# A buffer of zeros taken ahead of the first loads, and a copy of the turned sums cut in two

## The chip, the cores and the metric

One of the eight cores of a Trainium2 chip runs the whole kernel. The metric is the device time in microseconds (us), and the time before is the median of three runs. A core has five engines with a queue each: TensorE (PE, with its weight loads shown apart as PEld), VectorE (DVE), ScalarE (ACT), GpSimd (POOL) and SyncE (SP), which here only issues transfers. An engine takes its instructions in the order of its queue; engines wait for each other through semaphores.

## The reference

The kernel computes one layer of a Perceiver in float32: 256 latent tokens of width 512 read a context of 25,088 tokens of the same width, then attend to themselves, and then go through a mixture of 64 experts with a shared one. Cut to what matters here:

```python
qp = layernorm(x) @ Wq.T + bq           # 256 x 128
kp = ctx @ Wk.T + bk                    # 25088 x 128
z  = sigmoid(qp @ kp.T / sqrt(128))     # 256 x 25088
x  = x + z @ (ctx @ Wv.T + bv)
x  = x + attention(layernorm(x))        # 16 heads, causal
x  = x + experts(layernorm(x))          # top 8 of 64, and a shared expert
```

The kernel sums `z @ ctx` first and multiplies by `Wv.T` once at the end, so the sums over the context (called `zc`, 256 x 512) have to be turned (transposed) before that last product.

## The kernel before, in words

**Stages.** The context is read in 66 groups: group 0 has 128 tokens, the others 384 (three blocks of 128). The steady loop over the groups takes the span from about 23 us to 556 us. After it come the turn of the sums and the product with `Wv` (to about 566 us), the self-attention (to about 623 us), and the experts (to the end).

**A group.** For group g, `load_context` (L125) brings the tokens into a `ctx` tile (five buffers in a ring) and `load_quarters` (L115) brings them once more in four transfers, laid out so that one instruction of VectorE, `turn` (L315), makes the transposed `cT`. `keys` (L345) makes `kT` from `cT` on TensorE, `scores` (L365) makes the sigmoid `zT`, and `values` (L558) multiplies `zT` with the context into six PSUM banks `xacc`. That product runs through a scheme with fewer multiplications than the plain one; its sums and differences `S` and `T` are made by VectorE, GpSimd and ScalarE. Groups 0 and 1 are turned by TensorE instead (`turn_by_pe`, L319, tile `ptc`), because there is no time yet for the other layout.

**The start.** SyncE issues, in this order: half of `x`, `ctx` of group 0, `wk_plain`, `ctx` of group 1, four `quarters` of group 2, four parts of `wkT`, `ctx` of group 2, and then the groups that follow. Its later transfers wait for earlier ones to land, and, once the buffers are used up, for a buffer to come free. When `x` is there, VectorE computes mean and variance (`bn_stats`, L256), the reciprocal (L585) and the normalised `xn` in two halves of 128 tokens (L587). TensorE then turns `ctx` of group 0 (L332), turns `xn` (`pt_xn`, L598, eight transposes), makes the keys of group 0 (`pk`, L353) and the queries (`pq`, L611).

**The products of zeros.** `keep_warm(3)` (called at L581) multiplies a buffer of zeros `idle_sb` by itself three times; in float32 each product is two instructions, so six `pi` matmuls of 128 x 512. They stand first in TensorE's queue. The buffer of zeros is one of the five `ctx` buffers, filled by a memset of VectorE (L241).

**Order.** A scheduler may move instructions of an engine's queue unless they are wrapped in `in_turn`, which holds them in the order of the program among each other. The memset of L241 and the products of `keep_warm` are not wrapped. In the program the memset stands behind the loads and the constants and ahead of the statistics of `x`; in the queue of VectorE that the scheduler made it stands behind both halves of `xn`.

**The turn of the sums.** After the last group VectorE combines the banks into `zc` (L684), whose last thirds come one after another. `turn_zc(t, ...)` (L696) turns the half `t` of `zc`: four transposes on TensorE into a PSUM bank `pt_zc` (L700), then one copy of 128 x 512 by ScalarE into `zcT` (L705). `project_values` (L722) multiplies `zcT` with `Wv`, two instructions for each of the four chunks c. The calls stand in this order, which `in_turn` keeps:

```python
turn_zc(0, sum_bank)
project_values(0, range(0, 2))
turn_zc(1, sum_bank)
project_values(0, range(2, ND))
project_values(1, range(ND))
```

Of the kernel before, what the change touches and what calls it, by code (L numbers as in the profile page):

```python
# [9 lines left out]
F32 = mybir.dt.float32  # L10
# [4 lines left out]
P = 128  # L15
# [6 lines left out]
def tile_perceiver_layer(  # L22
# [25 lines left out]
    nc = tc.nc  # L48

    T, D = x.shape  # L50
# [9 lines left out]
    ND = D // P  # L60
    NI = I // P
    J = 3
# [13 lines left out]
    cpool = cross.enter_context(tc.tile_pool(name="cpool", bufs=2))  # L76
# [5 lines left out]
    def keys_bank(name):  # L82
        return psum.tile([P, 512], F32, tag="keys", name=name)
# [3 lines left out]

    def sum_bank(name):
        return pacc.tile([P, 512], F32, tag="acc", name=name)

# [104 lines left out]
        17: [fetch_lnog, fetch_lnob, fetch_gates],  # L197
    }


    ident = const.tile([P, P], F32, tag="ident", name="ident")
    make_identity(nc, ident)
# [33 lines left out]
    eps2_sb = const.tile([P, 1], F32, tag="eps2", name="eps2_sb")  # L236
    nc.vector.memset(eps2_sb, EPS * EPS)


    idle_sb = cpool.tile([P, J, D], F32, tag="ctx", name="idle_sb", bufs=5)[:, 0, :]  # L240
    nc.vector.memset(idle_sb, 0.0)  # L241

    def keep_warm(n):
        pi = keys_bank("pi")
        for _ in range(n):
            nc.tensor.matmul(pi, lhsT=idle_sb[:, 0:P], rhs=idle_sb, start=True, stop=True)

    in_turn = tc.keep_in_program_order  # L250

    def moments(src, nm, twice=False):

# [65 lines left out]
    def turn_by_pe(g):  # L319

        cT = new_turned(g)
        blocks = blocks_of(g)
        n = len(blocks)

        many = 512 // (n * P)
        for lo in range(0, ND, many):
            pt = sum_bank(f"ptc_{g}_{lo}")[:, 0 : many * n * P]
            for c in range(lo, lo + many):
                for i, k in enumerate(blocks):
                    at = ((c - lo) * n + i) * P  # L330
                    in_turn(
                        nc.tensor.transpose(  # L332
                            pt[:, at : at + P],
                            ctx_tiles[g][:, k, c * P : (c + 1) * P],
                            ident,
                        )
                    )
            to = cT[:, lo : lo + many, 0 : n * P // R, :]
            src = pt.rearrange("p (c b r) -> p c b r", c=many, r=R)
            if lo % 2:  # L340
                in_turn(nc.vector.tensor_copy(to, src))
            else:
                in_turn(nc.scalar.copy(to, src))
# [140 lines left out]
    def open_products():  # L484
        for i, names in enumerate(PRODUCTS):
            held = sum_bank(f"xacc_{i}")
            banks_of_products.append(held)
            at = 0
            for text in names:
                nm = text.split()[0]  # L490
                width = (WIDTH if nm in WIDE else WIDTH - 2) + (nm in WITH_ONES)
                product[nm] = (i, slice(at, at + width))
                at += width
            assert at <= 512
# [3 lines left out]
    for i in range(2):  # L498
        t = cpool.tile([P, NT_SUMS, WIDTH + 2], F32, tag=f"T{i}", name=f"T_{i}", bufs=1)
# [58 lines left out]
    def values(named, lo=0, hi=15):  # L558
# [7 lines left out]
        for i, (nm, lhs, rhs), last in made[lo:hi]:  # L566
# [12 lines left out]
            opened.add(i)  # L579

    keep_warm(3)  # L581
    xn = work.tile([P, NT, D], F32, tag="tok", name="xn")
    found = [moments(x_sb[:, t, :], f"x{t}") for t in range(NT)]
# [7 lines left out]
    turn_by_pe(0)  # L591
    xnT = work.tile([P, ND, T], F32, tag="tokT", name="xnT")
    pxs = [sum_bank(f"pt_xn_{c}") for c in range(0, ND, 2)]
    for t in range(NT):
        for c in range(ND):
# [13 lines left out]
    for c in range(ND):  # L609
# [3 lines left out]
                lhsT=wqT_sb[:, c, :],  # L613
                rhs=xnT[:, c, :],
                start=(c == 0),
                stop=(c == ND - 1),
# [45 lines left out]
    for i in range(len(PRODUCTS) - 1):  # L662
        n = max(cols.stop for b, cols in product.values() if b == i)
# [12 lines left out]
    for line in RESULTS.strip().splitlines():  # L676
        to, x_, op, y_ = line.split()
        a_, b_, o_ = result(x_), result(y_), result(to)
        n = widths[to] = min(widths[x_], widths[y_])
        assert to not in ("c01", "c11") or n == WIDTH  # L680
        if to[0] == "c" and to[2] != "1":
            n = WIDTH - 2
# [11 lines left out]
    zcT = work.tile([P, ND, T], F32, tag="tokT", name="zcT")  # L694

    def turn_zc(t, where):  # L696
        pt = where(f"pt_zc_{t}")
        for c in range(ND):
            in_turn(
                nc.tensor.transpose(  # L700
                    pt[:, c * P : (c + 1) * P], zc[:, t, c * P : (c + 1) * P], ident
                )
            )
        in_turn(
            nc.scalar.copy(  # L705
                zcT[:, :, t * P : (t + 1) * P], pt.rearrange("p (c q) -> p c q", c=ND)
            )
        )

    turn_zc(0, sum_bank)  # L710
    x1 = act.tile([P, NT, D], F32, tag="x1", name="x1")
    for t in range(NT):
# [21 lines left out]
# [5 lines that stand above are left out]
# [827 lines left out]
```

## Time and profile before

| What | Value |
|---|---|
| Median of three runs | 792.94 us (791.81 to 792.98) |
| The profiled execution's own time | 792.2 us |
| Its span on the core | 790.3 us |
| TensorE busy | 769.8 us (97% of the span) |
| VectorE, ScalarE, GpSimd busy | 548.3, 202.3, 154.4 us |
| Moved by DMA | 140.86 MB |

The span runs from the first to the last instruction of the profiled execution; 1.9 us of its time lie outside it. Times inside the span, such as 8.28 us, are counted from its start. "Busy" of TensorE includes the products of zeros.

### The profile page before, as it was taken

Reading aid. Unit: us, or ns where it says so; the run is one execution under the profiler, and the core shown is the slowest. Engines: PE = TensorE matmul, PEld = TensorE weight load, DVE = VectorE, ACT = ScalarE, POOL = GpSimd, SP = SyncE. Lnnn points to the kernel's source line nnn. Section 1 sums busy time; section 2 is a strip of 40 time slices with the busy share of each in tenths; the row PEclk is TensorE's granted clock in tenths of the full one; section 3 lists DMA queues with packets and bytes.
Section 4 is the critical chain, followed back from the end, with each engine's and each line's share of the span. In section 5 each row is a group of like instructions: output and inputs, shape, how many; then the busy total and the mean of one; then the engine's idle time right before and its main releaser. Section 6 shows DMA issues by size and latency. Waiting matters only on the chain.

```text
span 790.3 us, 12132 instructions
## 1 busy us (share of the span) xinstructions
PE 769.8 (97%) x4004; PEld 611.3 (77%) x4004; DVE 548.3 (69%) x1596; ACT 202.3 (26%) x483; POOL 154.4 (20%) x304
## 2 busy tenths in 40 slices
PE   5999999999999999999999999999999999999996
PEld 4788888888888888888888888888675586775562
DVE  3888887888878888788887888877656563513222
ACT  3322222222222222222222222222535210110110
POOL 2123232222322223222232222322124000000000
PEclk9999999999999999999999999999999999999999
DMA  9989999999879787786787878840510043399400
GB/s 247 254 213 229 269 230 270 224 230 219 190 181 213 170 210 187 187 209 169 210 186 185 209 171 208 187 121 1 193 47 2 1 133 121 122 353 391 158 1 30
DMA packets 153653, 140.86 MB, mean 178 GB/s; under 512 B 9072, under 2 KB 113008, under 8 KB 153584
## 3 DMA queue, kind: packets, MB, share of 16 engines
q1 hardware_dynamic: 152848, 139.49, 69.6%
q8 instruction: 34, 0.56, 0.3%
q10 hardware_dynamic: 672, 0.52, 0.2%
q14 instruction: 35, 0.29, 0.1%
q0 software_dynamic: 64, 0.00, 0.0%
HBM read 139.47 MB, written 0.52 MB: 177 GB/s over the span
## 4 chain that ended last, share of the span: by engine, by line
PE 95%; DVE 2%; ACT 1%; DMA 0%; POOL 0%; issue 0%; ACTq 0%
PE xacc L570 36%; PE pk L353 21%; PE pz L371 11%; PE ph_e L1124 7%; PE pd_e L1171 4%; PE ph_s L1124 3%; PE pd_s L1171 2%; PE pa L839 2%; PE ph_few L1393 1%; PE pw L903 1%; PE py L725 1%; PE ps L929 1%; PE ptp L980 1%; PE po_few L1424 1%; PE pf L1370 1%; PE pd_few L1438 1%
## 5 line engine op out<-in xcount | busy, mean ns | idle before, releaser
L570 PE MATMUL xacc<-T,S 128*128 128x172 f32 (+2 forms) x912 | 185.5, 308 | 0.0
L353 PE MATMUL pk<-cT,wkT_sb 128*128 128x384 f32 x512 | 175.5, 486 | 0.0
L570 PEld LDWEIGHTS xacc<-T,S 128*128 128x128 f32 x912 | 152.6, 190 | 20.3
L353 PEld LDWEIGHTS pk<-cT,wkT_sb 128*128 128x128 f32 x512 | 97.1, 190 | 54.4
L537 DVE TENSOR_TENSOR T<-ctx 128x172 f32<-128x172 f32 (+1 forms) x262 | 113.5, 434 | 0.0
L317 DVE STREAM_TRANSPOSE cT<-quarters 128x1536 f32<-128x1536 f32 x64 | 113.3, 1770 | 0.0
L537 POOL TENSOR_TENSOR T<-ctx 128x172 f32<-128x172 f32 x65 | 32.0, 493 | 391.3 <-PE xacc L570 373.5
L371 PE MATMUL pz<-qT,kT 128*128 128x256 f32 x392 | 106.0, 379 | 0.7 <-ACT kT L362 0.7
L537 DVE TENSOR_TENSOR S<-zT 128x128 f32<-128x128 f32 x196 | 56.2, 287 | 72.7 <-ACT zT L380 72.7
L380 ACT ACTIVATE zT<-pz 128x256 f32<-128x256 f32 (+1 forms) x131 | 64.2, 490 | 114.0 <-PE pz L371 114.0
L570 PE MATMUL xacc<-T,zT 128*128 128x173 f32 (+1 forms) x396 | 89.9, 308 | 0.0
L570 PE MATMUL xacc<-ctx,S 128*128 128x172 f32 x392 | 78.5, 309 | 0.0
L537 DVE TENSOR_TENSOR S<-zT,S 128x128 f32<-128x128 f32 x325 | 76.3, 284 | 0.0
L362 ACT ACTIVATE kT<-pk,bk 128x384 f32<-128x384 f32 (+1 forms) x66 | 38.2, 578 | 146.9 <-PE pk L353 146.9
L547 ACT COPY T<-ctx 128x170 f32<-128x170 f32 (+1 forms) x130 | 43.2, 334 | 125.4 <-PE xacc L570 125.4
L537 POOL TENSOR_TENSOR T<-ctx,T 128x170 f32<-128x170 f32 (+1 forms) x130 | 72.4, 576 | 2.2 <-PE xacc L570 2.2
L371 PEld LDWEIGHTS pz<-qT,kT 128*128 128x128 f32 x392 | 68.6, 190 | 4.8 <-ACT kT L362 1.3
L537 DVE TENSOR_TENSOR T<-ctx,T 128x172 f32<-128x172 f32 x195 | 65.5, 361 | 8.2 <-PE xacc L570 1.5
L570 PEld LDWEIGHTS xacc<-T,zT 128*128 128x128 f32 x396 | 66.4, 190 | 0.1
L570 PEld LDWEIGHTS xacc<-ctx,S 128*128 128x128 f32 x392 | 62.8, 190 | 0.0
L570 PE MATMUL xacc<-ctx,zT 128*128 128x170 f32 (+1 forms) x264 | 59.5, 307 | 0.0
L1124 PE MATMUL ph_e<-fT,gu 128*128 128x256 f32 x256 | 57.9, 381 | 0.0
(237 smaller groups left out, 713.2 us busy)
## 6 DMA issues: line engine op xcount, KB each, us to landing
ctx<-in_context SPq DMA_DIRECT2D x65, 768.0 KB, 5.3
quarters<-in_context SPq DMA_DIRECT2D x256, 192.0 KB, 6.3
gu<-in_e_gate_up SPq DMA_DIRECT2D x12, 1024.0 KB, 8.9
dn<-in_e_down SPq DMA_DIRECT2D x11, 512.0 KB, 7.0
gu_s<-in_s_gate_up SPq DMA_DIRECT2D x8, 512.0 KB, 6.4
a_wqT<-in_a_wqT SPq DMA_DIRECT2D x1, 2048.0 KB, 12.4
a_wout<-in_a_woutT SPq DMA_DIRECT2D x1, 2048.0 KB, 10.6
dn_s<-in_s_down SPq DMA_DIRECT2D x4, 512.0 KB, 7.8
```

The costliest lines, as they stand in the source:

```text
L317: in_turn(nc.vector.transpose(new_turned(g), q.rearrange("p b (c r) -> p c b r", r=R)))
L353: nc.tensor.matmul(pk, lhsT=w[:, c, :], rhs=cT[:, c, 0 : n // R, :].rearrange("p b r -> p (b r)"), start=(c == 0), stop=(c == ND - 1),)
L362: in_turn(nc.scalar.activation(kT[:, 0:n], pk, AF.Identity, bias=bk_sb))
L371: nc.tensor.matmul(pz[:, i * T : (i + 1) * T], lhsT=kT[:, at : at + P], rhs=qT, start=True, stop=True,)
L380: nc.scalar.activation(zT[:, blocks[0] : blocks[-1] + 1, :].rearrange("p j t -> p (j t)"), pz[:, 0 : len(blocks) * T], AF.Sigmoid, scale=1 ...
L537: in_turn(f(o_, a_, b_))
L547: in_turn(nc.scalar.copy(named[to][:, 0:n], named[x_][:, 0:n]))
L570: nc.tensor.matmul(banks_of_products[i][:, cols], lhsT=named[lhs], rhs=named[rhs][:, 0:n],  start=i not in opened, stop=(g == G - 1 and last),
L725: nc.tensor.matmul(pys[t], lhsT=zcT[:, c, t * P : (t + 1) * P], rhs=wvT_sb[:, c, :], start=(c == 0), stop=(c == ND - 1),)
L839: nc.tensor.matmul(pa[:, 0 : hi - lo], lhsT=a_wqT_sb[:, c, e * P : (e + 1) * P], rhs=anT[:, c, lo:hi], start=(c == 0), stop=(c == ND - 1),)
L1124: nc.tensor.matmul(ph[:, f * T + lo : f * T + hi], lhsT=gu[:, c, col : col + P], rhs=fT[:, c, lo:hi], start=(c == 0), stop=(c == ND - 1),)
L1171: nc.tensor.matmul(pd, lhsT=hT[:, f, t * P : (t + 1) * P], rhs=dn[:, f, :], start=(f == 0), stop=(f == NI - 1),)
```

## The change

Two edits. In the first, the buffer of zeros is taken from the ring of `ctx` buffers, and filled, at the head of the kernel, before any load of context is stated; the memset and the products of `keep_warm` are now held in the order of the program by `in_turn`. In the second, ScalarE's copy of the turned sums is made in two copies of 128 x 256 instead of one of 128 x 512, for each of the two halves t.

```diff
+    in_turn = tc.keep_in_program_order
+    idle_sb = cpool.tile([P, J, D], F32, tag="ctx", name="idle_sb", bufs=5)[:, 0, :]
+    in_turn(nc.vector.memset(idle_sb, 0.0))
...
+    def keep_warm(n):
+        pi = keys_bank("pi")
+        for _ in range(n):
+            in_turn(
+                nc.tensor.matmul(pi, lhsT=idle_sb[:, 0:P], rhs=idle_sb, start=True, stop=True)
+            )
...
-    idle_sb = cpool.tile([P, J, D], F32, tag="ctx", name="idle_sb", bufs=5)[:, 0, :]
-    nc.vector.memset(idle_sb, 0.0)
-
-    def keep_warm(n):
-        pi = keys_bank("pi")
-        for _ in range(n):
-            nc.tensor.matmul(pi, lhsT=idle_sb[:, 0:P], rhs=idle_sb, start=True, stop=True)
-
-    in_turn = tc.keep_in_program_order
...
-        in_turn(
-            nc.scalar.copy(
-                zcT[:, :, t * P : (t + 1) * P], pt.rearrange("p (c q) -> p c q", c=ND)
-            )
-        )
+        pc = pt.rearrange("p (c q) -> p c q", c=ND)
+        for c in range(0, ND, 2):
+            in_turn(
+                nc.scalar.copy(zcT[:, c : c + 2, t * P : (t + 1) * P], pc[:, c : c + 2, :])
+            )
```

In the queues that result, the memset is the first instruction of VectorE, where it was the one behind the second half of `xn`; the order on TensorE, GpSimd and SyncE is the one of before, and ScalarE has four copies of `zcT` where it had two.

## The prediction

> **What bounds the kernel now.** I read the page first. TensorE is busy in nearly every slice of the span, but not in the first.
>
> ```profile
> span 790.3 us, 12132 instructions
> ...
> PE   5999999999999999999999999999999999999996
> ...
> PE 95%; DVE 2%; ACT 1%; DMA 0%; POOL 0%; issue 0%; ACTq 0%
> ```
>
> The second line gives TensorE's busy share in 40 slices of 19.8 us, the third the engines' shares of the chain that ended last. TensorE sets the end nearly everywhere, so time is won where it stands still or does something useless on that chain. The list of TensorE's waits has one that outweighs the rest:
>
> ```profile
> PE pi L246 <- DVE idle_sb L241: 8.3, 1, 8.3
> ```
>
> TensorE waits 8.3 us for the buffer of zeros; the next entry is 0.9 us, and between 25 and 556.5 us the list is empty. So a shift at the start isn't given back to a wait that is in the loop already. The chain of waits of the first 25 us (start us, us, what) shows what stands around it:
>
> ```profile
> 0.76 3.91 DMA x_sb<-in_x
> ...
> 7.14 0.55 DVE xn L587
> 7.68 0.06 issue
> 7.74 0.50 DVE idle_sb L241
> 8.23 0.04 issue
> 8.28 4.72 PE pi L246 x6
> 13.00 0.44 PE ptc L332 x4
> 13.43 0.87 PE pt_xn L598 x8
> 14.31 0.96 PE pk L353 x8
> ```
>
> The real work could start when xn is there, at 7.69. Instead the memset follows xn, the six products of zeros follow the memset, and the first transposes start at about 12.9. The whole 4.72 us of products of zeros lies on the chain. The other edit touches the stretch behind the loop, seen in the timeline (start us, us, engine, line, out<-in):
>
> ```profile
> 557.71 0.70 PE L700 MATMUL pt_zc<-ident,zc 128*128 128x128 f32 x4 [0.70 <-DVE zc L684]
> ...
> 558.45 0.59 ACT L705 COPY zcT<-pt_zc 128x512 f32<-128x512 f32 x1 [1.40 <-PE pt_zc L700]
> ...
> 559.08 1.98 PE L725 MATMUL py<-wvT,zcT 128*128 128x512 f32 x4 [0.68 <-ACT zcT L705]
> ...
> 560.18 0.33 DVE L684 TENSOR_TENSOR zc<-u 128x172 f32<-128x172 f32 x1
> ```
>
> TensorE stands still for 0.68 us while ScalarE copies all four chunks, of which the next four instructions need two.
>
> [...] the first pi products follow each other in 0.85 us, the sixth starts 0.55 us behind the fifth, and the products after it in 0.43 us; if the clock doubled once, it was at 12.1, or 3.83 us after the first. [...] between 556.86 and 559.08 TensorE runs only four transposes, and the products behind them start 0.43 us apart, at full clock.
>
> **Edit 1, the zeros.** Nothing is removed or added but waits; one memset moves from behind xn to the head of VectorE's queue. The queues of SyncE, GpSimd and ScalarE keep their order and waits here, so no transfer is moved past another: ctx of group 4 still is what takes the buffer of zeros over, and it was issued at 19.24, after the buffer had been free for 6 us.
> - Memset: VectorE's first instruction starts at 0.83, so it runs from 0.83 to 1.31 (0.48 us, its row). Behind it stand seven small memsets, done at 1.33 before and then at 1.8; the next work, the statistics of x, waits for x until 4.70. This cover is 2.9 us, so the memset costs nothing.
> - Products of zeros: from 1.37 (the same 0.06 us behind the memset) for 4.72 us, to 6.09, while TensorE would wait anyway.
> - ptc (0.44 us): ctx of group 0 landed at 5.5, so it follows at about 6.0 and ends at 6.5. ScalarE copies it from 6.75 (behind the second square root, which ended at 6.72) to 7.35.
> - pt_xn: the second half of xn is done at 7.69; with 0.14 us from VectorE to a transpose (557.56 to 557.71 in the loop's end) its four transposes start at 7.83, and the last at 8.16. Before, that one started at 14.04. **Shift: 14.04 - 8.16 = 5.88 us.** From there pk, pq and the copies follow in the order and with the gaps of before.
>
> Does the data arrive 5.88 us earlier? The trace's transfers (size, us from issue to landing):
>
> ```profile
> ctx<-in_context SPq DMA_DIRECT2D x1, 768.0 KB, 8.1
> quarters<-in_context SPq DMA_DIRECT2D x1, 192.0 KB, 8.5
> ```
>
> Those are ctx of group 1, issued at 2.15, landing at 10.2, and the last quarter of group 2, issued at 5.21, landing at 13.75. Needed are, in the new times: wk_plain (landed 7.3) at 8.3; ctx of group 1 at 16.83 - 5.88 = 10.95; the quarters of group 2 by the turn at 19.51 - 5.88 = 13.6, which slips by 0.1 us but whose keys are wanted at 18.7, 3 us after it is done; wkT (landed 15.05) at 18.7; ctx of group 2 (17.1) at 18.5; the quarters of group 3 (20.7) at 21.6; those of group 4 (26.3) at 27.9. All are there, by 0.7 us at the closest. None of these issues moves, as they wait for each other; from about 28 us on the issues of before were tied to freed buffers and move along. So all 5.88 us should stay.
>
> **Edit 2, the copies.** One copy of 128x512 (0.59 us) becomes two of 128x256. A row of that shape and engine is there, in the timeline of the experts' part:
>
> ```profile
> 629.74 0.37 ACT L287 COPY fT<-pt_fn 128x256 f32<-128x256 f32 x1 [1.52 <-PE pt_fn L279]
> ```
>
> The first copy still waits for all four transposes (the second has no wait of its own), so the first products start 0.59 - 0.37 = **0.22 us** earlier, at 558.86, and end their issue at 560.68 instead of 560.90. The transposes of the other half need zc, whose last sum ends at 560.51; with 0.14 us, 560.65, so the gain just stays. The second copies end 0.15 us later (2 x 0.37 - 0.59), under 1.7 us of products; for half 1 they end at about 562.1, while its products start at 562.85. Half 0's x1 and all after it follow TensorE. If the last sum comes later, the gain is 0; if TensorE pays for the added waits, up to -0.1 us.
>
> **Sum.** 5.88 + 0.22 = 6.1 us. Against the profiled execution: 792.2 - 6.1 = 786.1. The median of the runs is 0.74 us above that execution. [...] Between 786.1 and 792.94 - 6.1 = 786.8 I take **786.5**.
>
> **The rivals.**
> - *The clock falls back or comes late* (0.13). Between 6.0 and 8.3 TensorE then runs 12 transposes in 2.3 us, where it had dense work before. [...] Against it speaks the stretch at 557 us. The price is 1 us for each us of work at half clock[...]. If it is only late, 0.5 us: 787.0.
> - *The data comes late* (0.03). The closest margin is 0.7 us, while the DMA engines are full until about 31 us. If the loop's start hangs on landings, the whole gain is lost, as if TensorE were at the same place at 25 us: 792.7, no change. Against: the margins above.
> - *The clock stays low: slower* (0.02). Place: pk, pq and the first groups, in the start. To eat 6.1 us and 1.6 us more, 7.7 us of work must run at half clock, i.e. until about 8.3 + 15.4 = 23.7. That is the deciding point; at 30 us it would be 6.1 - 10.9 = -4.8 us, 797.7. Against: the work is dense from 8.3 on, and the clock of before rose after 3.83 us.
> - *The zeros don't come ahead* (0.02): then only 0.22 us remain, 792.7, no change. Against: the memset has no wait and is first in the queue.
>
> **The numbers.** The main case has 0.80, and 785.3 to 787.6. A difference within 0.2% (1.6 us) can hardly be told from no change. Faster: 0.80 + 0.13 + part of the data case, 0.95; same: 0.03; slower: 0.02. The range, 785.2 to 789.3, takes in the main case and most of the clock's.
>
> **What would show it.** Right: pi starts at about 1.4 and pq at 9.2 (15.1 before), the turn of group 3 at 21.6; the first pi waits 1.4 us instead of 8.3; the copy row shows 0.37 us x4 and py starts 0.45 us behind the end of the transposes. Wrong: transposes 0.21 us apart or pk 0.21 us apart instead of 0.11; a wait of TensorE for ctx or of VectorE for quarters before 25 us; zeros still at 8 us.

## The result, and the profile after

The changed kernel takes 785.78 us (median of four runs, 785.58 to 786.78), the kernel before 792.46 us beside it (the three runs of the table and one more): a ratio of 0.9919, with a 95% interval of 0.9901 to 0.9936. The profiled execution took 785.86 us with a span of 784.0 us, against 792.2 and 790.3 us, so 6.3 us less in both. The forecast was 786.5 us for the median and 786.1 for the profiled execution.

The chain of waits of the first 12 us after the change (start us, us, what):

```profile
0.93 0.50 DVE idle_sb L96
1.43 0.04 issue
1.47 5.08 PE pi L211 x6
6.55 0.44 PE ptc L334 x4
6.99 1.15 PE pt_xn L600 x8
8.14 0.89 PE pk L355 x8
9.03 1.73 PE pq L613 x8
```

The products of zeros now run from 1.47, while x and ctx are on their way, and the keys follow at 8 us instead of 14. VectorE's timeline shows the other end of that stretch, the second half of xn, which TensorE waits for last:

```profile
6.88 0.55 DVE L589 TENSOR_SCALAR xn<-x_sb,mv_x,rs_x 128x512 f32<-128x512 f32 x1
```

It ends at 7.43, and the last four transposes start at 7.48. The transposes ahead of them, of the first half, started 7.215 at the latest and could be followed at 7.32: TensorE stood still here for 0.16 us. So the zeros, which run without a gap until 6.39, and the path of x end almost together. The list of TensorE's waits, with what was waited for (us in total, times, longest us), has become:

```profile
PE pi L211 <- DVE idle_sb L96: 1.5, 1, 1.5
...
PE py L727 <- ACT zcT L709: 0.5, 1, 0.5
```

8.3 us became 1.5. How far each later step moved, from the same instructions in both traces: the first pq instruction from 15.11 to 8.87 (6.23 us), all pz and all but one pk 6.23, the first transpose of zc from 557.71 to 551.47 (6.23), the first py product from 559.08 to 552.63 (6.45), the last product of the experts from 782.95 to 776.50 (6.45). So edit 1 gave 6.23 us and edit 2 gave 0.22 us, and no later stage gave anything back. The timeline of the turned sums after the change:

```profile
551.47 0.70 PE L702 MATMUL pt_zc<-ident,zc 128*128 128x128 f32 x4 [0.70 <-DVE zc L686]
...
552.21 0.65 ACT L709 COPY zcT<-pt_zc 128x256 f32<-128x256 f32 x2 [1.40 <-PE pt_zc L702]
...
552.63 1.98 PE L727 MATMUL py<-wvT,zcT 128*128 128x512 f32 x4 [0.46 <-ACT zcT L709]
```

TensorE waits 0.46 us for the first of the two copies, where it waited 0.68 us for the one. The two copies overlap: 0.65 us for both, not 2 x 0.37.

### The profile page after: what moved, and what is told of

The parts are those of the page before. It is cut to its first block, busy times and chain, and to the rows that moved or that the text cites. A ratio compares the mean times of both kernels' runs of the same rounds, so it can differ in the third digit from the quotient of the medians.

```text
span 784.0 us, 12134 instructions
## 1 busy us (share of the span) xinstructions
PE 770.4 (98%) x4004; PEld 611.3 (78%) x4004; DVE 547.4 (70%) x1596; ACT 202.4 (26%) x485; POOL 154.3 (20%) x304
## 4 chain that ended last, share of the span: by engine, by line
PE 96%; DVE 2%; ACT 1%; POOL 0%; issue 0%; ACTq 0%
PE xacc L572 36%; PE pk L355 22%; PE pz L373 11%; PE ph_e L1126 7%; PE pd_e L1173 4%; PE ph_s L1126 3%; PE pd_s L1173 2%; PE pa L841 2%; PE ph_few L1395 1%; PE pw L905 1%; PE py L727 1%; PE ps L931 1%; PE ptp L982 1%; PE po_few L1426 1%; PE pf L1372 1%; PE pd_few L1440 1%
```

## The experiments

**The zeros alone.** The changed kernel with the copy in one piece (the lines are shortened here and below):

```diff
-        for c in range(0, ND, 2):
-            in_turn(nc.scalar.copy(zcT[:, c : c + 2, ...], pc[:, c : c + 2, :]))
+        in_turn(nc.scalar.copy(zcT[:, :, t * P : (t + 1) * P], pt.rearrange(...)))
```

> The changed kernel with ScalarE's copy in one piece again, so edit 1 alone. If the shift at the start makes nearly the whole gain, the products of zeros start at about 1.5 us and everything from the queries (pq) on lies 6.2 us earlier than before; the time is 6.2 us under the kernel before, 0.2 us over the changed kernel. Rival: the copies made a good part of the gain; then the time is more than 1 us over the changed kernel.

Measured: 785.79 us, against 791.88 us of the kernel before on that chip (ratio 0.9924, 0.9910 to 0.9937). Edit 1 is the gain, as far as times can tell; the 0.2 us of edit 2 don't show between medians. The trace of this run agrees: the loop, the first product of the turned sums and the last product of the experts all lie 6.1 us earlier than before.

**The copies alone.** The kernel before with the copy in two halves:

```diff
-        in_turn(nc.scalar.copy(zcT[:, :, t * P : (t + 1) * P], pt.rearrange(...)))
+        for c in range(0, ND, 2):
+            in_turn(nc.scalar.copy(zcT[:, c : c + 2, ...], pc[:, c : c + 2, :]))
```

> The kernel before with ScalarE's copy in two halves, so edit 2 alone. If only the wait for the first half counts, the first py product starts 0.45 us behind the end of the transposes instead of 0.68, all that follows lies 0.22 us earlier, and the time is within 0.2% of before (-0.2 us). Rival: the transposes of the other half wait for the last sum of zc, and the 0.22 us are given back there: no shift at the first product of the other half.

Measured: 791.88 us against 791.88 us (ratio 0.9998, 0.9989 to 1.0006). In its timeline the first product follows 0.46 us behind the end of the transposes:

```profile
558.18 0.70 PE L700 MATMUL pt_zc<-ident,zc 128*128 128x128 f32 x4 [0.70 <-DVE zc L684]
559.35 1.98 PE L725 MATMUL py<-wvT,zcT 128*128 128x512 f32 x4 [0.46 <-ACT zcT L707]
```

Counted from the first transpose of zc, the product behind the second half's transposes comes after 3.42 us, against 3.63 us before. So the gain of 0.21 us is kept past the other half's transposes, and the rival falls. It is below what times can show.

**The ring or the order?** Edit 1 does two things: it takes the buffer earlier, and it holds the memset in order. Here neither is done; only the buffer is changed, in the kernel before, at the old line:

```diff
-    idle_sb = cpool.tile([P, J, D], F32, tag="ctx", name="idle_sb", bufs=5)[:, 0, :]
+    idle_sb = cpool.tile([P, D], F32, tag="idle", name="idle_sb", bufs=1)
```

> The kernel before, with one edit: the buffer of zeros has a place of its own in the pool of context, outside the ring of five ctx buffers, and stays at its old line, with no order imposed. In the queue that results, VectorE's memset stands in fifth place among the constants. Theory: what kept the memset late was that its buffer stood in the ring behind the first loads; then the zeros start at about 1.6 us, and the time is about 6 us under before, like edit 1 alone. Rival: the order held by hand, or the ring's buffer taken first, is needed for the gain: then the zeros start later or transfers wait, and the time is like before, 792.5.

Measured: 785.75 us (ratio 0.9924, 0.9909 to 0.9939), the gain of edit 1. VectorE's timeline has the memset among the constants, at its old line 241:

```profile
0.95 0.06 DVE L237 MEMSET eps_sb<- 128x1 f32 x1
1.06 0.48 DVE L241 MEMSET idle_sb<- 128x512 f32 x1
1.51 0.18 DVE L500 MEMSET T<- 128x60 f32 x2
```

So the scheduler put the memset late because its buffer came from the ring of the loads; neither another line nor `in_turn` was needed, and the kernel could have kept all else. That the buffer's place in the ring behind those of the first loads was the reason is likely, but not shown by itself, and neither is which of the two parts of edit 1 is needed while the buffer stays in the ring.

**No zeros.** The changed kernel without the line `keep_warm(3)`:

```diff
-    keep_warm(3)
```

> The changed kernel without the products of zeros (the memset stays). TensorE's first work is then the transposes of ctx of group 0, at about 5.2 us. Theory: the products of zeros bring the clock up, at 6.0 us in the trace after; without them the transposes and pk start at half clock (0.21 us apart instead of 0.11), [...] and the time is 1.4 to 3.1 us over the changed kernel. Rival: the clock comes up anyway by the time that the work is dense, or the zeros only fill a wait: no change against the changed kernel, within 0.5 us.

Measured: 787.43 us, 4.5 us under the kernel before on that chip (ratio 0.9946, 0.9936 to 0.9956), and 1.65 us over the changed kernel by the medians; the 1.4 to 3.1 us forecast were the author's estimate. (One of the 14 runs took 791.94 us, the others 786.51 to 788.04; what held that one up isn't on record.) Its timeline of TensorE:

```profile
6.81 1.97 PE L599 MATMUL pt_xn<-ident,xn 128*128 128x128 f32 x8 [0.43 <-DVE xn L588]
8.57 1.92 PE L355 MATMUL pk<-cT,wk_plain 128*128 128x128 f32 x8
10.28 2.00 PE L612 MATMUL pq<-xnT,wqT 128*128 128x256 f32 x8
```

The eight transposes take 1.76 us to the start of pk, 0.21 us each, and so does pk; the first pq pair is 0.33 us apart and the others 0.22, so the clock rose at about 10.5. The trace also records the clock that TensorE is granted, and there full speed begins at 10.49. So the zeros are worth about 1.7 us, but only where they are hidden. In the kernel before they lay on the chain for 4.72 us. This run is that kernel without its zeros, but for the 0.2 us of edit 2 and a memset that nothing waits for: without them the kernel before would have been faster by an estimated 4.3 us (4.5 - 0.2).

**Six zeros.**

```diff
-    keep_warm(3)
+    keep_warm(6)
```

> The changed kernel with six products of zeros instead of three. In the trace after, the zeros end 0.16 us ahead of what the second half of xn allows, at 6.39 by start of the next transposes. Theory: the zeros are hidden only up to there; six more instructions at full clock, 0.43 us each, push the first transposes to 9.0 and pk from 7.98 to 10.3: 2.3 us over the changed kernel. Rival: there is slack in the start (the wait for x), and under 1 us is added.

Measured: 787.27 us (ratio 0.9941, 0.9924 to 0.9957), 1.5 us over the changed kernel. The profiled execution took 788.79 us and has the clock rising at about 7.6 instead of 6.0, so its pk starts at 11.07, 3.1 us later than in the changed kernel. Of these 0.8 us are the clock's 1.6 us of half speed, and 2.3 the six instructions. The other runs lie at 787.0 to 787.4; when their clock rose isn't on record, so the smaller cost there is not explained. An early rise would do for much of it: 3.8 us behind the first zero, as in the kernel before, so at 5.3, it would save an estimated (7.6 - 5.3) / 2 = 1.15 us. The forecast of 2.3 us was too high for the median, but the rival, under 1 us, falls as well.

**Two zeros.**

```diff
-    keep_warm(3)
+    keep_warm(2)
```

> The changed kernel with two products of zeros instead of three. They end at about 4.9 us at half clock; then come the transposes of group 0 from 5.3 to 6.2 and those of xn from 6.8. Theory: [...] the clock comes up between 6 and 8 us, and 0 to 0.8 us are added to the changed kernel. Rival: [...] the clock comes up as late as without zeros (10.5): 1.6 us over the changed kernel.

Measured: 785.84 us (ratio 0.9923, 0.9906 to 0.9939): no difference to three. In its timeline the transposes of ctx are still 0.21 us apart (from 5.36), those of xn 0.11 us (from 6.90):

```profile
5.36 1.08 PE L334 MATMUL ptc<-ident,ctx 128*128 128x128 f32 x4
6.90 1.31 PE L600 MATMUL pt_xn<-ident,xn 128*128 128x128 f32 x8 [0.46 <-DVE xn L589]
```

The clock rose between 6.0 and 7.1, a stretch in which TensorE stood still for 0.46 us: the wait for xn is now that long, and the path of x sets the start. So the third product is not needed here.

**Late data, after and before.** The same exchange in the changed kernel and in the kernel before:

```diff
-    load_context(1)
     load_quarters(2)
+    load_context(1)
```

> The changed kernel with the load of ctx of group 1 behind the four quarters of group 2 instead of ahead of them, so that it lands at about 13.7 us instead of 10.4. Theory: the shift has used up the slack of the data: TensorE wants this tile at 10.6 and waits about 3.2 us for it; half of the gain is lost, 3.2 us over the changed kernel. Rival: the data has slack in the new kernel too, and nothing changes.

> The kernel before with the same exchange: ctx of group 1 behind the quarters of group 2, landing at about 13.7 us. TensorE wants it at 16.8 there. Theory: 3 us of slack cover it, and the time is that of before, within 0.3 us. Rival: the exchange itself costs (the sums that GpSimd makes of this tile, or transfers behind it): about 3 us over before, as in the changed kernel.

Measured: 790.22 us in the changed kernel (ratio 0.9975, 0.9968 to 0.9981), 4.4 us over it; 792.37 us in the kernel before (ratio 1.0003, 0.9994 to 1.0012), no change. So the shift used up slack of the data that the kernel before had, as expected, but the cost is 1.2 us over the forecast. TensorE's timeline of the first shows why:

```profile
13.57 2.71 PE L334 MATMUL ptc<-ident,ctx 128*128 128x128 f32 x12 [2.58 <-DMA ctx<-in_context]
16.07 1.06 PE L373 MATMUL pz<-qT,kT 128*128 128x256 f32 x2
16.93 2.85 PE L355 MATMUL pk<-cT,wk_plain 128*128 128x384 f32 x8
```

Twelve transposes that took 1.47 us in the changed kernel take 2.71 us: the first two are 0.16 us apart, as behind other waits at full clock, the rest 0.21. The wait of 2.6 us is followed by work at half clock. The clock did not fall in every run: in six of the 20 the mean granted clock is 0.998, and they took 788.17 to 789.50 us; in the other 14 it is 0.996 or 0.997, and they took 790.07 to 791.65 us. The medians of the two groups lie 1.6 us apart.

**The wait filled.** That kernel with products of zeros in the wait:

```diff
+    keep_warm(3)
     turn_by_pe(1)
     open_products()
```

> The run with the late tile in the changed kernel (ctx of group 1 behind the quarters of group 2), with three more products of zeros between pq and the turn of that tile. In that run TensorE waited 2.6 us for the tile, then ran the twelve transposes 0.21 us apart instead of 0.11 and the first scores 0.43 us apart. Theory: the wait let the clock fall to half, which cost some 1.6 us on top of the wait; the zeros fill the wait (six at 0.43 us), the transposes keep 0.11 us, and the time is 1.3 to 1.8 us under the run with the late tile, about 788.6. Rival: what followed was slow for another reason (the landing transfers, the sums), and filling the wait changes nothing: 790.2.

Measured: 788.58 us (ratio 0.9957, 0.9943 to 0.9971), 1.64 us under the run without them. The transposes start at 13.41 at full clock:

```profile
10.65 2.83 PE L211 MATMUL pi<-idle_sb 128*128 128x512 f32 x6
13.41 1.53 PE L334 MATMUL ptc<-ident,ctx 128*128 128x128 f32 x12
```

So of the 4.4 us, 2.8 are the wait and 1.6 the clock that fell in it. The runs of the late tile that kept their clock say the same: they took as long as these.

**A bank for each pair.** The changed kernel with the first copy waiting for two transposes:

```diff
     def turn_zc(t, where):
+        for c in range(0, ND, 2):
+            pt = where(f"pt_zc_{t}_{c}")
...
+            in_turn(nc.scalar.copy(zcT[:, c : c + 2, t * P : (t + 1) * P], pc))
```

> The changed kernel, with the turned sums of each pair of chunks in a PSUM bank of its own, so that the first copy waits for two transposes instead of four. The trace after has the first copy at 552.21, 0.04 us behind the end of the fourth transpose, while the second ended at 551.95. Theory: the first copy starts at about 551.99, and the first py product 0.2 us earlier than in the changed kernel, about 0.23 us behind the end of the fourth transpose; the time is 0.2 us under the changed kernel. Rival: the bank after the first is not free in time, or the last sum of zc (ends at 554.27) holds the transposes of the other half: the first product is earlier, but the second half's products aren't.

Measured: 785.36 us (ratio 0.9916, 0.9903 to 0.9930). TensorE's timeline:

```profile
552.08 0.70 PE L703 MATMUL pt_zc<-ident,zc 128*128 128x128 f32 x4 [0.70 <-DVE zc L686]
553.03 1.98 PE L727 MATMUL py<-wvT,zcT 128*128 128x512 f32 x4 [0.24 <-ACT zcT L710]
```

From the first transpose to the first product it takes 0.95 us, against 1.16 after and 1.38 before; the product behind the second half's transposes comes after 3.20 us, against 3.42. It is the fastest of all in the median, by 0.4 us; the trace accounts for 0.2 of them, and the intervals overlap, so that it beats the changed kernel is shown by the trace and not by the times.

## Why the prediction was right

- **The bound.** TensorE's wait for the zeros, and the 4.72 us of zeros on the chain, were the loss; the loop had no wait that could take the gain back. The last products of the experts lie as much earlier (6.45 us) as the first product of the turned sums.
- **The shift, 5.88 us forecast, 6.23 measured.** The step from xn to the transposes was taken as 0.14 us and was 0.05, and x landed at 4.42 instead of 4.67. Together 0.34 us, which is the difference (two gaps between the instructions behind, of 0.06 and 0.07 us, cancel). The landing of x is scatter: over seven profiled executions (before, after, the copies alone, no zeros, two zeros, and the late data after and before) it lies between 4.40 and 4.67, and the profile of before had the latest. So most of what the shift has over the forecast is chance; a forecast from one execution carries such a term with it.
- **The zeros, 4.72 us forecast, 5.08 measured** (the row of the chain; up to the next transpose, 4.92, from 1.47 to 6.39), as the clock rose 4.54 us behind their start instead of 3.82, and half of that difference (0.36 us) is lost. It hardly counted, because they end 0.16 us ahead of what xn allows. By the prediction's own steps 0.9 us were left there (the eight transposes ahead of 7.83 need 0.87 us, so they could begin at 6.96, and were to begin at 6.0). That was too much: the zeros ended 0.4 us later, and the transposes of xn could end 0.35 us earlier; six zeros showed that three more are not hidden.
- **Memset at the head of VectorE.** Right: it starts at 0.93, and the small memsets behind it end at 1.83, 2.6 us ahead of x.
- **The data.** Right in that TensorE didn't wait for a transfer, but the closest margin was thinner than the 0.7 us forecast: ctx of group 1 landed at 10.4 and was wanted at 10.6. The turn of group 2 moved by 5.67 us only, since its quarters landed at 13.76, and its keys were 2.7 us away. One thing wasn't foreseen: the turn of group 18 waited 1.15 us for its quarters, a wait that VectorE didn't have in the loop of the kernel before, nor with the zeros alone, the own buffer, two zeros or two banks. TensorE didn't see it, 2.5 us being left to the keys. And one of the prediction's signs of being wrong did appear, without harm: ahead of 25 us, VectorE stood still for 0.48 us before the turn of group 2, which began 0.08 us behind the landing of its quarters.
- **Edit 2, 0.22 us forecast, 0.22 measured.** The row of another copy of that shape priced it well. The wait for all four transposes was read rightly, and the version with two banks shows its price, another 0.22 us. The forecast that the second copies end 0.15 us later was wrong: two copies of this kind overlap, and both take 0.65 us.
- **The rivals.** The clock did not fall back after the change: transposes are 0.11 us apart throughout. But such a loss exists: without zeros, where the clock rose at 10.49 instead of 6.01, the time is 1.7 us longer, and in the run with the late tile, where it fell behind a wait of 2.6 us, the fall costs 1.6 us. How long it would last here, and so the room left for it in the forecast range, was the author's estimate. The mild form, a clock that is only late, came up as well, at the 0.5 us forecast or a little over: in the profile of the two banks the clock rose about 6.2 us behind the first zero instead of 4.54, and pq began 0.6 us later than in the changed kernel. The data rival exists as well, and only 0.2 us kept it away: with the tile 3.1 us later (13.5 instead of 10.4) two thirds of the gain were lost.
- **The median, 786.5 us forecast, 785.78 measured.** The kernel before measured 792.46, 791.88, 791.93 and 792.02 us beside the various runs, below the 792.94 from which the forecast was taken; with the 6.45 us of the traces these give 785.4 to 786.0.

## What to carry to other kernels

In this kernel, work that only warmed TensorE was free as long as it ended ahead of the first real operand: three products of zeros, which ended 0.16 us ahead of what xn allowed, cost nothing against two (785.78 and 785.84 us), and six cost 1.5 us. Compare both ends, and ask what the filling of its buffer waits for. Where a scheduler orders the queues, the buffer that an instruction takes can decide its place: a small buffer outside the ring of the loads gave here the same 6 us as the reordering. A shift at the start costs slack of the data, and a wait that comes back can be dearer than its length: here 2.8 us of wait made the time 4.4 us longer, as TensorE's clock fell in it.

## What the runs showed of the hardware

- **The clock can fall in a wait of 2.6 us.** In the run with the late tile half clock began within 0.2 us of the first transpose behind the wait, and full speed came back at about 17.1, 3.4 us later. By the mean granted clock this happened in 14 of the 20 runs; why the other six kept full speed was not shown. Three stretches of the trace show it (window, its length, busy us of PE, PEld, DVE, ACT and POOL with their instructions, then the granted clock: 1.00, 0.50, 1.00; the last two columns are of DMA):

```profile
6.90:13.70 6.80, 4.22 (x30) 3.63 (x29) 1.68 (x3) 2.92 (x5) 0.04 (x1) 1.00 1.17 274
13.72:17.13 3.41, 3.41 (x15) 3.23 (x15) 1.37 (x4) 0.96 (x2) 1.81 (x4) 0.50 1.11 295
17.14:24.00 6.86, 6.19 (x26) 4.22 (x26) 4.96 (x13) 2.40 (x6) 0.98 (x2) 1.00 1.18 270
```

- **The clock did not rise at the same time in every trace.** It rose 3.8 us behind the first product of zeros in the trace before, 4.5 us behind it after, and about 5.0 us (the copies alone), 5.8 us (the late data before) and 6.2 us (the two banks) in others; what set this was not shown. In the kernel before, the zeros on the chain carried this scatter into the time: with a rise 3.8, 5.0 and 5.8 us behind the first zero (before, the copies alone, the late data before) pq began at 15.1, 15.6 and 15.9. In the changed kernel, where the zeros are hidden, pq began at 8.87 with a rise after 4.5 us; with the rise after 6.2 us, in the two banks, it began 0.6 us later.
- **A rise behind transposes.** Without zeros, full speed began at 10.49, 5.2 us behind the first transpose. In between TensorE made twelve transposes, in 3.05 us, and products of pk for 1.7 us, and stood still for 0.4 us. So the clock rose although the larger part of the work ahead of it was float32 transposes.
